# Transformer block with a routed feed-forward on one core: rate and waits of the indirect DMAs in the slots' stage

## The chip, the core and the metric

The kernel runs on one NeuronCore of a Trainium2 chip. The core has five instruction streams that run side by side and meet at semaphores: TensorE (PE, matmuls and transposes), VectorE (DVE), ScalarE (ACT), GpSimd (POOL) and SyncE (SP, which here issues the plain DMAs). Transfers are carried by 16 DMA engines that all queues share. The metric is the device time of one execution in microseconds (us). The kernel before takes 2183.7 us, the median of 12 runs from 2173.35 to 2190.69.

## What is computed

16 sequences of 512 tokens with 128 features pass through one block: layer norm with a modulation per sequence, causal attention with 16 heads of 8, and a feed-forward part with 160 experts of which each token uses 8. Cut to the part that the change bears on:

```python
logits = x @ router_w.T + expert_bias
probs = sigmoid(logits)
top_w, top_idx = top_k(probs, 8)
top_w = top_w / (sum(top_w) + 1e-09) * 2.5
combine = zeros((T, 160)).at[arange(T)[:, None], top_idx].set(top_w)
h1 = silu(einsum('th,eih->eti', x, w_gate))       # 64 inner features
routed = einsum('eti,ehi->th', h1 * combine.T[:, :, None], w_down)
shared = silu(x @ w_gate_shared.T) @ w_down_shared.T
return routed + shared
...
x = x + gb * ffn(h)
```

All arithmetic on the main path is in 32 bit; the scores of the attention use sums of bf16 parts.

## The kernel before

The kernel has two stages. In the first, up to about 1120 us of the profiled execution, it runs the attention of all 16 sequences, and behind it the routing: which expert gets which token, and in which place. In the second, the slots' stage, the experts are applied.

**Slots.** The sequences are taken in eight groups (`GROUPS = (2, 3, 3, 2, 2, 2, 1, 1)`). In each group every pair of experts gets blocks of 128 slots in two tensors in HBM: `xg`, the inputs by slot, and `yg`, the outputs by slot. Four blocks make a quad, and the stage works quad by quad, 28, 36, 36, 28, 28, 28, 22 and 22 of them by group, 228 in all (a few more of each group are kept in reserve and stand in a branch, `spare_quads`, L868 to L881, that every engine tests once a group at L870 and L874). For one quad SP loads `xs` from `xg` (L797), TensorE transposes it (`turn`), `up` multiplies by the first weights (`wq`, copied from a resident table by ACT and DVE, two blocks each), ACT applies silu, `down` multiplies by the second weights (`wd`, L814), ACT copies the result to `y`, and SP stores it to `yg` (L864).

**Indirect DMAs.** Two kinds go between tokens and slots, each with 128 rows of 512 bytes and each issued by GpSimd. A scatter (`scattering`, L752) writes 128 tokens' rows into `xg`; a sequence has 4 blocks of tokens times 8 choices, 32 of them, and all 16 have 512. A gather (`gathering`, L975) reads, for 128 tokens and one of their choices, the rows of `yg` into a slice of the tile `got`; there are 512 of these too. When the eight gathers of a block of tokens are there, `combine` (L987 to L999) weights and adds them on VectorE in six instructions, and after the fourth block SP stores the sequence to the output. `got` has five buffers (`LAG + 2`).

**What sets the order.** PE, SP, ACT and DVE run in the order of the source; GpSimd's side work and indirect DMAs are put into one order by `in_order`. Every indirect DMA also goes through `paced`, which adds a wait for `steps.last`, the matmul or transpose that stands last in the source at that point. In the attention the `Pacer` asks for one indirect DMA each 1.3 us of the planner's clock (`PACE`). In the slots' stage the loop at L1181 goes quad by quad; after each quad's steps it adds `RATE` to a debt (L1205) and issues one indirect DMA for each whole unit of it, scatters first, then gathers (L1207, `stream`). Nothing to issue sets the debt to zero. A group's gathers are put into the queue when the `down` of its last quad has been issued (L1200 to L1202). `add_up` (L1172) then issues the combines, keeping the three newest blocks back (`LAG`). `prepare_sums` (L1161) starts the shared expert (`shared_expert`, L886) and the top-8 weights (`weights`, L920) of the sequences whose gathers come next, on PE's tile `o`, ACT and DVE. What is left of the gathers after the last quad is issued by the loop at L1209.

`moe.sb` is None until the attention has ended, and is set at L1149, ahead of the quad loop.

Of the kernel before, what the change touches and what calls it, by code (L numbers as in the profile page):

```python
# [38 lines left out]
LAG = 3  # L39


PACE, RATE = 1.3, 2.3
PERIOD = 1.25


# [26 lines left out]
def block_kernel(ctx: ExitStack, tc: tile.TileContext, t: dict, out: bass.AP):  # L72
# [22 lines left out]
    steps = Steps()  # L95
# [128 lines left out]
    def in_order(ins):  # L224
        if behind:
            tc.add_manual_dep(ins, behind[-1].name, NO_SYNC, reason="order of issue")
        behind.append(ins)

    def paced(ins):

        if steps.last is not None:
            tc.add_manual_dep(ins, steps.last.name, SYNC, reason="pace")
        in_order(ins)

# [507 lines left out]
    def scattering():  # L742

        while True:
            while not next_rows:
                look_ahead()
                yield None
            gr, i, h = next_rows.popleft()
            look_ahead()
            for j in range(NBLK):  # L750
                for k in range(TOPK):
                    s = nc.gpsimd.indirect_dma_start(  # L752
                        out=gr.xg,
                        out_offset=bass.IndirectOffsetOnAxis(
                            ap=gr.idx[:, NBLK * i + j, k : k + 1], axis=0
                        ),
                        in_=h[:, j, :],
                        in_offset=None,
                    ).ins
                    tc.declare_no_dep(s, group=f"scatter{gr.g}", reason="every slot once")  # L760
                    tc.add_to_no_dep_group(f"scatter{gr.g}", s)
                    paced(s)
                    left[gr.g] -= 1
                    yield s
# [3 lines left out]
    moe = SimpleNamespace(sb=None)  # L768
# [198 lines left out]
    def gathering():  # L967

        while True:
            while not gathers:  # L970
                yield None
            gr, i, j = gathers.popleft()
            got = moe.sb.tile([P, TOPK, D], FP, tag="got", name="got", bufs=LAG + 2)
            for k in range(TOPK):
                s = nc.gpsimd.indirect_dma_start(  # L975
                    out=got[:, k, :],
                    out_offset=None,
                    in_=gr.yg,
                    in_offset=bass.IndirectOffsetOnAxis(
                        ap=gr.idx[:, NBLK * i + j, k : k + 1], axis=0  # L980
                    ),
                ).ins
                paced(s)
                yield s
            sums.append((gr, i, j, got))
# [445 lines left out]
```

## Time and profile before

| | |
|---|---|
| median of 12 runs | 2183.7 us (2173.35 to 2190.69) |
| the profiled execution | 2178.5 us |
| its span, first to last instruction | 2176.7 us |
| mean granted TensorE clock | 0.897 |
| busy, of the span: PE, DVE, ACT, POOL | 77%, 54%, 49%, 52% |
| scatters (L752): count, busy, mean of one | 512, 495.0 us, 967 ns |
| gathers (L975): count, busy, mean of one | 512, 511.4 us, 999 ns |
| first gather, last gather (start) | 1252.2 us, 2156.9 us |
| first and last `turn` transpose (start) | 1125.4 us, 1985.8 us |

Times in the trace are counted from the span's first instruction. "Busy" leaves out waiting. A row of a wait names who ended it: "A <- B" is time that A stood idle until B was done, as the profile infers it from the semaphores. The granted clock is what the throttle gave TensorE, as a share of full speed. The profile gives the DMA engines' load as the mean busy share of the 16. "issue" is time in which the engine waited for nothing that the profile shows.

### The profile page before, as it was taken

The page shows a single profiled execution, that of the slowest core. Times are in us where ns is not written, and L with a number is a line of the kernel's source. Part 1 is how long each engine was busy: PE and PEld are TensorE (multiplying, and loading weights), DVE is VectorE, ACT ScalarE, POOL GpSimd, SP SyncE. Part 2 cuts the span into 40 slices and gives each one's busy share as a digit, 9 for nine tenths or more (in the row PEclk, how much of TensorE's full clock was granted, in tenths as well). Part 3 has the DMA queues.
Part 4 walks back from the last instruction along what each step waited for, and adds up shares of the span by engine and source line. Part 5 has one row for each costly group of instructions (what it writes and reads, how often), then busy time and mean ns, then how long its engine had stood idle before and what let it go on. Part 6 is the DMA issues. An engine that isn't in the chain of part 4 may idle for free. (4 is left out here: it accounts for less than half of the span.)

```text
span 2176.7 us, 39288 instructions
## 1 busy us (share of the span) xinstructions
PE 1670.3 (77%) x12248; PEld 1127.2 (52%) x12248; DVE 1180.6 (54%) x3153; ACT 1066.8 (49%) x2031; POOL 1139.0 (52%) x1139
## 2 busy tenths in 40 slices
PE   2899987988879888788868888887978887887100
PEld 1455544544445444444447677676767676766000
DVE  2787776776667666565623313245454544454633
ACT  1466554654455444544556655555555555654000
POOL 4011066226654556666515555565666565656775
PEclk8899999998999898998989999999999999997555
DMA  3456555555555565565588788788888888887211
GB/s 98 130 178 187 165 182 176 175 167 169 185 183 168 180 212 166 172 196 178 180 276 265 249 260 275 250 271 288 271 266 281 266 281 263 293 266 234 82 56 43
DMA packets 298149, 445.30 MB, mean 205 GB/s; under 512 B 44923, under 2 KB 168796, under 8 KB 297920
## 3 DMA queue, kind: packets, MB, share of 16 engines
q1 hardware_dynamic: 265152, 375.32, 53.3%
q0 software_dynamic: 32768, 67.17, 10.7%
q8 instruction: 113, 1.85, 0.4%
q14 instruction: 116, 0.95, 0.1%
HBM read 223.37 MB, written 218.17 MB: 203 GB/s over the span
## 5 line engine op out<-in xcount | busy, mean ns | idle before, releaser
L752 POOL DMA_INDIRECT xg<-hs,idx x512 | 495.0, 967 | 401.1 <-PE s L105 146.2
L975 POOL DMA_INDIRECT got<-yg,idx x512 | 511.4, 999 | 288.7 <-issue 116.2
L1234 DVE TENSOR_REDUCE mins<-s 128x2 f32<-128x1024 f32 (+3 forms) x448 | 396.7, 912 | 231.4 <-PE s L105 174.3
L1234 ACT ACTIVATE pT<-s 128x1024 f32<-128x1024 f32 x320 | 322.0, 1021 | 254.8 <-PE s L105 180.8
L105 PE MATMUL down<-wd,su 128*128 x1824 | 274.0, 295 | 97.4 <-issue 46.3
L105 PEld LDWEIGHTS down<-wd,su 128*128 128x128 f32 x1824 | 229.7, 197 | 169.8 <-issue 106.8
L105 PE MATMUL up<-xT,wq 128*128 128x128 f32 x1824 | 257.5, 287 | 2.5 <-issue 2.5
L105 PE MATMUL s<-krep,qrep 96*128 96x512 bf16 (+3 forms) x1024 | 204.8, 314 | 67.0 <-issue 22.3
L105 PE MATMUL s<-qrep,krep 128*128 128x512 bf16 (+3 forms) x1024 | 202.5, 312 | 57.5 <-ACT pT L1234 25.2
L1234 DVE COPY wq<-wg 128x128 f32 x456 | 90.7, 251 | 278.4 <-PE up L105 179.2
L105 PEld LDWEIGHTS up<-xT,wq 128*128 128x128 f32 x1824 | 238.6, 204 | 2.6 <-issue 2.6
L105 PE MATMUL av<-pT,v 128*32 128x512 f32 (+3 forms) x2048 | 206.9, 470 | 0.6 <-issue 0.6
L1234 ACT ACTIVATE su<-up 128x512 f32<-128x512 f32 x228 | 137.4, 603 | 128.2 <-PE up L105 89.5
L1234 ACT COPY y<-down 128x512 f32<-128x512 f32 x228 | 133.4, 585 | 120.1 <-issue 35.9
L237 POOL TENSOR_TENSOR rot<-rot,three 128x512 f32<-128x512 f32 x32 | 36.7, 1159 | 279.3 <-ACT three L1234 279.1
L105 PEld LDWEIGHTS <-qrep 96*128 96x128 bf16 x1024 | 84.1, 100 | 175.4 <-issue 137.6
L105 PEld LDWEIGHTS <-identb 128*128 128x128 bf16 x1280 | 124.9, 102 | 89.6 <-issue 14.2
L1234 ACT COPY xT<-turn 128x512 f32<-128x512 f32 x228 | 133.2, 584 | 77.4 <-issue 26.3
L112 PE MATMUL turn<-ident,xs 128*128 128x128 f32 x912 | 148.6, 289 | 21.9 <-DMA xs<-xg 18.7
L105 PEld LDWEIGHTS <-krep 128*128 128x128 bf16 x1024 | 89.0, 100 | 104.8 <-issue 85.8
L1234 ACT COPY wq<-wg 128x128 f32 x456 | 114.1, 299 | 38.5 <-issue 21.5
L112 PEld LDWEIGHTS turn<-ident,xs 128*128 128x128 f32 x912 | 112.4, 149 | 39.3 <-issue 33.8
(174 smaller groups left out, 2218.8 us busy)
## 6 DMA issues: line engine op xcount, KB each, us to landing
xg<-zeros SPq DMA_DIRECT2D x288, 256.0 KB
xs<-xg SPq DMA_DIRECT2D x228, 256.0 KB
wd<-in_wdT SPq DMA_DIRECT2D x228, 256.0 KB
yg<-y SPq DMA_DIRECT2D x228, 256.0 KB
krep<-parts SPq DMA_DIRECT2D x64, 288.0 KB
qrep<-parts SPq DMA_DIRECT2D x192, 96.0 KB
yg<-zeros SPq DMA_DIRECT2D x60, 256.0 KB
parts<-three SPq DMA_DIRECT2D x96, 128.0 KB
```

The source lines that it names most:

```text
L105: steps.last = nc.tensor.matmul(out_, lhsT=lhsT, rhs=rhs, start=start, stop=stop).ins
L112: steps.last = nc.tensor.transpose(out_, in_, ident).ins
L237: in_order(getattr(nc.gpsimd, op)(*args).ins)
L752: s = nc.gpsimd.indirect_dma_start(out=gr.xg, out_offset=bass.IndirectOffsetOnAxis(ap=gr.idx[:, NBLK * i + j, k : k + 1], axis=0), in_=h[: ...
L975: s = nc.gpsimd.indirect_dma_start(out=got[:, k, :], out_offset=None, in_=gr.yg, in_offset=bass.IndirectOffsetOnAxis(ap=gr.idx[:, NBLK * i ...
L1234: return getattr(self.engine, op)(*args, **kwargs)
```

## The change

Two lines. The rate of the quad loop goes from 2.3 to 2.9 indirect DMAs a quad. And `paced` adds its wait for TensorE only while `moe.sb` is None, that is in the attention; in the slots' stage an indirect DMA keeps the order of its queue and its waits for data, and has no other.

```diff
-PACE, RATE = 1.3, 2.3
+PACE, RATE = 1.3, 2.9
...
     def paced(ins):
 
-        if steps.last is not None:
+        if moe.sb is None:
             tc.add_manual_dep(ins, steps.last.name, SYNC, reason="pace")
         in_order(ins)
```

## The prediction

> **What bounds the kernel now.** I read the slices of the page first, then busy time by stretches, then the waits of TensorE and GpSimd in the slots' stage, then the timeline of the end. The profiled execution took 2178.5 us around a span of 2176.7; the median of the 12 runs is 2183.7, 5.2 above it. The sum below is made in the span and carried to the median with 1.8 + 5.2 = 7.0.
>
> ```profile
> PE   2899987988879888788868888887978887887100
> POOL 4011066226654556666515555565666565656775
> ```
>
> Each digit is 54.4 us. From slice 20 on the slots run, with PE at 8 to 9 tenths and POOL at 5 to 6; in the last three slices PE is gone and POOL alone goes on at 7.
>
> ```profile
> core 0: us, PE busy (x) PEld busy (x) DVE busy (x) ACT busy (x) POOL busy (x), PEclk, DMA share, GB/s
> 1250.00:1990.00 740.00, 621.27 (x4369) 525.24 (x4368) 329.50 (x1010) 419.76 (x1015) 445.88 (x451) 0.95 0.84 271
> 1990.00:2115.00 125.00, 24.30 (x88) 15.57 (x86) 64.20 (x150) 7.39 (x15) 94.28 (x93) 0.52 0.30 89
> 2115.00:2177.00 62.00, 0.00 (x0) 0.00 (x0) 22.41 (x50) 0.00 (x0) 33.04 (x33) 0.50 0.15 44
> ```
>
> Between 1250 and 1990 PE is busy 84%, POOL issues 451 indirect DMAs, and the DMA engines are 84% busy. After 1990 there are 126 more, with PE and the DMA engines nearly idle: this end is GpSimd's alone.
>
> ```profile
> PE down L105 <- issue: 43.2, 43, 2.5
> PE down L105 <- ACT y L1234: 25.5, 18, 3.6
> PE down L105 <- DMA xs<-xg: 3.9, 2, 2.0
> PE up L105 <- DMA hides<-hide: 3.1, 2, 1.8
> PE down L105 <- DMA wd<-in_wdT: 2.2, 1, 2.2
> POOL got L975 <- PE up L105: 81.8, 66, 2.9
> ```
>
> These are waits in 1250 to 1990 (us in total, times, longest). TensorE lost about 10 us to transfers and none to a gather, so PE's own chain sets the stage. GpSimd lost 81.8 us in this line alone to the pacing wait. 784 `turn` matmuls, four a quad, lie in that stretch: 196 quads in 740 us, 3.78 us a quad.
>
> ```profile
> 1991.38 11.41 SPq L864 DMA_DIRECT2D yg<-y  x4
> 2005.93 0.94 POOL L975 DMA_INDIRECT got<-yg,idx  x1 [1.73 <-PE o L112]
> 2115.79 0.94 POOL L975 DMA_INDIRECT got<-yg,idx  x1 [0.30 <-DVE got L1234]
> 2156.85 0.94 POOL L975 DMA_INDIRECT got<-yg,idx  x1 [0.31 <-issue]
> 2141.12 1.23 DVE L1234 TENSOR_TENSOR got<-got,w 128x1024 f32<-128x1024 f32 x1
> 2149.51 1.23 DVE L1234 TENSOR_TENSOR got<-got,w 128x1024 f32<-128x1024 f32 x1
> 2166.31 1.23 DVE L1234 TENSOR_TENSOR got<-got,w 128x1024 f32<-128x1024 f32 x1
> 2169.78 1.22 DVE L1234 TENSOR_TENSOR got<-got,w 128x1024 f32<-128x1024 f32 x1
> ```
>
> Start, duration, idle before and what ended it. The instruction list has 116 gathers behind the last branch of L874. The trace has 116 starts from 2005.93 to 2156.85, so these are they: 1.31 us each, back to back. The last 32, from 2115.79, belong to the last group, whose results were all sent by 2002.8. They wait for nothing but the 84 gathers of older groups in front of them. A combine, the six VectorE instructions from one of these DVE lines to the next, takes 8.4 us at 2141 and 3.5 at 2166.
>
> **The change, part by part.** The instruction list of the changed kernel can be read without running it. Up to the slots' stage nothing differs, and there are as many matmuls, copies and DMAs in all. Behind the last branch stand 32 gathers, not 116. The other 84 move into the stage, with the shared expert (L886) and the weights (L920) of the last batches and their combines. All indirect DMAs from the start of the stage on lose their wait on PE and keep those on data: the landing of the group's `yg`, a free `got` buffer (five), the indirect DMA eight before.
>
> *The end.* The first gather of group 7 now needs only its `yg`. At the first group's end such a gather began at 1252.2, 5.9 us after its last `yg` DMA had been issued (to 1246.3). So here it begins at 2002.8 + 5.9 = 2008.7. The 32 then take what they take now up to the last start, 2156.85 - 2115.79 = 41.1, to 2049.8; 2 us to land; one combine of 3.5 to 8.4, since DVE has 10 us a block and is no longer two combines late; 3.5 us for the output, as from 2173.2 to 2176.7 now. That is 2059 to 2064; I take 2062, a gain of 115. If DVE stays as late as now, the span ends 60.9 behind the first of the 32, at 2069.6: 107.
>
> *TensorE.* The moved shared experts are 48 matmuls. At the end they take 17.33 us on a clock of 0.52; in the stage 72 such take 14.39 us, 0.20 each.
>
> ```profile
> 1750.00:1990.00 240.00, 14.39 (x72) 8.88 (x72) 3.43 (x5) 5.80 (x13) 0.96 0.86 277
> 1990.00:2115.00 125.00, 17.33 (x48) 9.65 (x48) 2.06 (x3) 4.33 (x9) 0.52 0.30 89
> ```
>
> (Columns as above for tile `o`, without POOL.) 48 x 0.20 = 9.6 us, all on the path, since PE sets the stage. Bounds: 0, if they fall into PE's gaps, and 17.3. ACT's share, 4.3 us, lies under PE at 57% busy. DVE gets some 60 us more (86.6 at the end now, less about 26 that stay); 329.5 of 740 rises by seven points to about 52%, hidden behind PE. Should that cover go, the price is one combine, 3.5 us, ahead of the `wq` copies, which are written two quads before their use: still hidden.
>
> *The DMA engines.*
>
> ```profile
> q1 hardware_dynamic: 265152, 375.32, 53.3%
> q0 software_dynamic: 32768, 67.17, 10.7%
> ```
>
> 10.7% of 2176.7 over 1024 indirect DMAs is 0.227 us of all 16 engines each: 84 x 0.227 = 19.1. Loads and stores of the moved batches, about 3.2 MB at 53.3% x 2176.7 / 375.32 = 3.09 us a MB, add 9.9. These 29 us go into an idle share of 0.16 x 740 = 118. If hidden they cost nothing; if the engines are the bound, 29. Nearest row: the 10 us that PE now waits for transfers. Idle share falls by a quarter, so I take 4 us more.
>
> *GpSimd.* A gather in the stage is 384.08 us / 387 = 0.99 us, and the next begins 0.30 later: 1.29. 2.9 x 1.29 = 3.74 us a quad against 3.78. It just keeps up while there is work (the first five groups, 156 of 228 quads). By the tail's 1.31 it is 3.80, 0.02 x 156 = 3 us late; I take 3. What is behind a late gather: the next gathers, then the combine, three blocks (24 gathers, 31 us) later in the list, then on DVE the `wq` copies and on SP the output at L999 and the loads behind it. The far end is the longest gather of the stage, 1.90 + 0.30; that is the slower rival.
>
> The wait itself I cost at nothing: a full GpSimd is behind PE's place, so pacing holds it seldom. The cover is that fullness; in groups 5 to 7 the list runs empty and only data holds it.
>
> The Trainium skill speaks against the change here: "SBUF — State Buffer", section "SBUF: two separate sides", says that VectorE's 32-bit copies inside SBUF lock GpSimd out of writing DMA descriptors. The two `wq` copies a quad (0.227 us median each) would add 0.45 us to 2.9 x 1.244 = 3.61, making 4.06 and costing 0.28 x 156 = 44 us. The rows of this case show a mean of 0.99 over a median of 0.944, 0.05 a gather, and the sum goes by them.
>
> Sum of the span: 2176.7 - 115 + 9.6 + 4 + 3 = 2078.3. With 7.0 for the median: about 2085.
>
> **Rivals.**
> *The forecast, about 2085, chance 0.68.* For it: PE waits for no gather, and the last 32 stand behind older ones.
> *Half is given back, chance 0.22.* DMA engines at 84% already have slices of nine tenths, so the added work could be fully exposed: 17.3 + 29 in place of 9.6 + 4, and a gain of 107 at the end. 2176.7 - 107 + 17.3 + 29 + 3 + 7 = 2126. Against it: only 10 us of PE's waits are for transfers.
> *Late gathers hold TensorE, slower, chance 0.08.* GpSimd falls behind by more than 31 us, the combine waits at the head of DVE, `wq` comes late, PE runs at GpSimd's rate. It decides from 2.9c = 3.78 + 98 / 156 (98 being what the rest gains, 115 less 9.6, 4 and 3), c = 1.52 us a gather. At c = 1.65 it is 4.79, 1.01 x 156 = 157 us: 2085 + 157 = 2242. For it: single gathers of 1.9, unpaced bursts. Against: bursts of five in the trace hold 1.25 to 1.3.
> *The waits' removal and the rate cancel, no change, chance 0.02.* Were the list emptied only on paper, GpSimd would keep its 0.61 DMAs a us, 451 / 740, and the 84 end as late as now: 2184. Against: 81.8 us of its waits are the pace.
>
> **How the numbers follow.** The low end is zero cost in the stage with the full 117 at the end: 2183.7 - 117 = 2067, rounded out to 2064. The high end is the half-back case with the gather at 1.31 and DVE late by one combine more, 2126 + 8 = 2134, to 2136. That leaves out the slower rivals and a little of each edge. A change within 0.3%, 6.5 us, can't be told from none. Faster: 0.68 + 0.22 = 0.90; same 0.02; slower 0.08.
>
> **What would show it.** Behind the last branch 32 starts of `got`, not 116, and PE's last matmul about 60 us before the end in place of 107. POOL at 7 tenths or more over slices 23 to 34, with no wait on PE there. PE's stage longer by 10 to 25 us. The prediction is wrong if a DVE wait on `got` stands in the stage, if a gather's mean there passes 1.2 us, or if PE's waits for `xs`, `wd` and `hides` grow past 40 us.

## The result, and the profile after

The changed kernel takes 2551.1 us (median of 15 runs, 2527.2 to 2561.3) beside 2180.6 us for the kernel before (62 runs), a ratio of 1.1695 [1.1672, 1.1718]. It is slower by 370 us, where 2085 us, a gain of about 99, was forecast. The profiled execution has a span of 2545.1 us at a mean granted clock of 0.830; before it was 2176.7 us at 0.897.

The page after, its rows of busy tenths (40 slices of 63.6 us):

```profile
PE   3899889888887788857460981865766666647561
POOL 3111462466266566533446036344444444554414
PEclk8899989998999899978785985877877778877776
```

Up to the slots' stage, which begins in the 18th slice, the rows are nearly those of before. From there on PE mostly has 4 to 7 tenths, in two slices 0 and 1, and the clock falls with it. GpSimd is not fuller but emptier: mostly 3 to 5 tenths where 7 were foreseen.

One view cut to windows of 20 us in the stage of the changed kernel (columns: window, length, busy time and instructions of PE, PEld, DVE, ACT and POOL, granted clock, DMA share, GB/s):

```profile
1320.00:1340.00 20.00, 1.19 (x8) 0.78 (x6) 0.89 (x3) 1.18 (x2) 15.29 (x16) 0.59 0.22 73
1340.00:1360.00 20.00, 1.89 (x9) 1.89 (x10) 0.00 (x0) 1.08 (x3) 15.19 (x16) 0.50 0.22 64
1360.00:1380.00 20.00, 2.81 (x14) 2.05 (x13) 0.00 (x0) 0.59 (x1) 15.12 (x16) 0.59 0.26 80
1380.00:1400.00 20.00, 0.00 (x0) 0.00 (x0) 0.36 (x2) 0.60 (x1) 8.51 (x9) 0.50 0.12 33
1400.00:1420.00 20.00, 17.77 (x127) 16.04 (x128) 3.68 (x19) 13.68 (x32) 0.00 (x0) 0.86 0.73 230
1420.00:1440.00 20.00, 20.00 (x147) 16.51 (x145) 3.36 (x16) 14.70 (x35) 0.00 (x0) 1.00 0.81 255
```

While GpSimd issues 16 indirect DMAs in 20 us, one every 1.25 us, matmuls, DVE and ACT together have under 4 us of work in the 20. When GpSimd holds still, PE is busy for 18 to 20 us at once. The DMA engines are not full in the first four windows, 0.12 to 0.26. So the stop is no lack of DMA bandwidth.

How a stop begins, in the timeline of the changed kernel (start, duration, instruction, and in brackets the idle time before it):

```profile
1136.07 0.96 POOL L752 DMA_INDIRECT xg<-hs,idx  x1 [0.30 <-issue]
...
1136.19 0.23 PE L105 MATMUL s<-digits,onesb 1*128 1x160 bf16 x1
1137.33 0.96 POOL L752 DMA_INDIRECT xg<-hs,idx  x1 [0.30 <-issue]
...
1144.60 0.82 DVE L1234 TENSOR_TENSOR key<-s,m 128x640 f32<-128x640 f32 x1 [13.20 <-issue]
```

The DMA at 1136.07 is the sixth of a run that began at 1129.74. DVE needs only the `s` that PE ended at 1136.4, and starts 8 us later.

The instructions by which SP issues the loads of `wd` (L814; duration in ns, minimum, median, maximum), of the changed kernel in the window 1355 to 1395:

```profile
L814 SPq FUSED_REGOPS  x1: 700/700/700, 1363.0 to 1363.0; - x1
L814 SPq MOVE wd<-in_wdT x1: 688/688/688, 1365.8 to 1365.8; - x1
```

Over the whole execution the median of the first is 37 ns, of the second 29. In these stretches a step of SP's sequencer, one that moves no data, takes 0.69 to 0.70 us. The kernel before has such steps too (its longest `FUSED_REGOPS` at L814 takes 703 ns). Of all 456 such steps at L814 in the changed kernel, 24 of the 71 that begin behind the sixth or a later indirect DMA of an unbroken row take 0.68 us or more, and 2 of the 385 others.

The longest waits of the changed kernel between 1125 and 2490 us (sum, times, longest):

```profile
DVE wq L1234 <- remote: 419.3, 32, 57.2
POOL got L975 <- DVE xr L1234: 371.1, 32, 66.2
...
PE down L105 <- ACT y L1234: 276.7, 36, 38.6
```

"remote" is a release that the profile can't name. The second row is GpSimd at the end of its runs (a run is a row of indirect DMAs with no gap to speak of between them): with no other wait it runs ahead until all five buffers of `got` are full, and is held by data alone. Its whole list of waits for PE, 81.8 us on `up` before, is gone as the change says.

### The profile page after: what moved, and what is told of

It reads as the page before. It is cut to its first block, busy times and chain, and to the rows that moved or that the text cites. A ratio compares the mean times of both kernels' runs of the same rounds, so it can differ in the third digit from the quotient of the medians.

```text
span 2545.1 us, 39051 instructions
## 1 busy us (share of the span) xinstructions
PE 1760.0 (69%) x12248; PEld 1209.1 (48%) x12248; DVE 1170.5 (46%) x3153; ACT 1082.5 (43%) x2031; POOL 1125.3 (44%) x1139
## 5 line engine op out<-in xcount | busy, mean ns | idle before, releaser
L975 POOL DMA_INDIRECT got<-yg,idx x512 | 496.3, 969 | 632.7 <-DVE xr L1234 371.1
L105 PE MATMUL down<-wd,su 128*128 x1824 | 316.5, 326 | 446.5 <-ACT y L1234 277.4
L105 PEld LDWEIGHTS down<-wd,su 128*128 128x128 f32 x1824 | 267.3, 225 | 521.2 <-ACT y L1234 294.8
L105 PE MATMUL up<-xT,wq 128*128 128x128 f32 x1824 | 282.5, 304 | 12.7 <-issue 12.1
L105 PEld LDWEIGHTS up<-xT,wq 128*128 128x128 f32 x1824 | 264.4, 222 | 9.1 <-issue 8.3
L112 PE MATMUL turn<-ident,xs 128*128 128x128 f32 x912 | 168.6, 316 | 41.1 <-DMA xs<-xg 19.3
L112 PEld LDWEIGHTS turn<-ident,xs 128*128 128x128 f32 x912 | 128.1, 165 | 68.2 <-issue 38.6
```

The costliest lines, as they stand in the source:

```text
L105: steps.last = nc.tensor.matmul(out_, lhsT=lhsT, rhs=rhs, start=start, stop=stop).ins
L112: steps.last = nc.tensor.transpose(out_, in_, ident).ins
L975: s = nc.gpsimd.indirect_dma_start(out=got[:, k, :], out_offset=None, in_=gr.yg, in_offset=bass.IndirectOffsetOnAxis(ap=gr.idx[:, NBLK * i ...
```

## The experiments

The experiments stand in four groups, and every result is a ratio to the kernel before, timed in the same group. The results name the chip. The first group ran on chip 4, where the kernel before took 1998 us; the second on chip 5 (2180 us); the third and fourth on chip 15 (2194 and 2196 us). Beside the runs of the changed kernel above it took 2181 us; the chip of those is not named. In brackets stands a 95% interval.

### One part of the change at a time, chip 4 (before: 1998.1 us)

The wait for PE's place given back, the rate kept:

```diff
-        if moe.sb is None:
+        if steps.last is not None:
```

> Rate 2.9 with the wait on TensorE kept. Theory A (it is GpSimd running ahead with nothing to hold it that stops the other engines, and the wait was what held it): the tail shrinks as forecast and nothing stops, 2085 to 2110 us. Theory B (the rate: back-to-back indirect DMAs stop the other engines whatever they wait for, and at 2.9 a quad they are back to back): slower than before, 2300 to 2550 us. Theory C (more gathers in the stage make DVE wait for late data): 2200 to 2400 us, with DVE waits on got in the stage.

Measured: 1908.2 us, 0.956 [0.952, 0.961].

The old rate, without the wait:

```diff
-PACE, RATE = 1.3, 2.9
+PACE, RATE = 1.3, 2.3
```

> Rate 2.3 without the wait on TensorE. Theory A: the gathers still go in bursts of eight and more, ahead of their place, so the other engines stop as in the changed kernel: 2400 us or more. Theory B: at 2.3 a quad there is idle time between them, so the stage stays as it was and the time is 2170 to 2200 us. Theory C: as B.

Measured: 1980.9 us, 0.992 [0.990, 0.995].

In two more, scatters keep the wait and each gather waits instead for the landing of the gather four (or three) before it. In this and the later diffs "..." stands for lines that are left out: `paced` gets a second argument, `gather`, which only the gathers set, and the lists begin empty.

```diff
...
-        if moe.sb is None:
+        if moe.sb is None or gather is None:
             tc.add_manual_dep(ins, steps.last.name, SYNC, reason="pace")
+        elif len(ring) >= 4:
+            tc.add_manual_dep(ins, ring[-4].name, SYNC, reason="depth")
+        if gather:
+            ring.append(ins)
...
```

> Rate 2.9, scatters wait for TensorE, a gather in the slots' stage waits for the landing of the gather four before it in place of TensorE (the semaphore lanes alone allow eight). Theory A in the form that the number of indirect DMAs handed over and not yet landed decides, with a threshold between four and eight: 2080 to 2120 us. Theory B, and theory A in the form that any run of gathers ahead of their place stops the others: 2400 us or more.

> As the run with four, with the gather three before it. Theory A by number in flight: no stops if four had none, and if four had some, fewer; three in some 4 us (0.96 to issue, 0.3, 2.7 to land) are 1.33 us a gather, about full rate, so 2090 to 2150 us. Theory B: as the run with four, 2400 us or more.

Measured: 0.979 [0.974, 0.984] and 1.0225 [1.0175, 1.0275].

In these runs the loss is not there. The same step at L814, of the kernel with rate 2.9 and the wait kept, is never slow:

```profile
L814 SPq FUSED_REGOPS  x228: 37/37/51, 1022.0 to 1845.9; - x114
```

The same 37/37/51 stands in all four traces, the one without the wait among them, in which GpSimd's longest run has 122 indirect DMAs without a break (gaps under 0.5 us). A depth of three holds GpSimd itself, which is why it loses; the gathers' row of that kernel on its page:

```profile
L979 POOL DMA_INDIRECT got<-yg,idx x512 | 523.2, 1022 | 289.3 <-DMA got<-yg,idx 178.9
```

There, late gathers do what the prediction's slower rival said. None of the theories on the wait could be decided here; their times in us were set for a kernel before of 2180 us.

### The changed kernel again, and the wait by kind of DMA (before: 2179.7 us)

The changed kernel without an edit, then the kernel with the wait and the new rate of above:

> The changed kernel itself, once more, beside the kernel before of the same call. Two theories are left after four runs in which the kernel before took 1998 us, where it had taken 2181 us beside the changed kernel's 2551 us. Theory C (the chip): the stop of the other engines comes on chips that are slower already under the kernel before, and unheld GpSimd only sets it off there. Then, if before takes about 2000 us in this call, the changed kernel takes 0.94 to 0.99 of it (the kept-wait kernel's 0.956, and the 0.992 of the kernel without wait at the old rate, set its ends), the register operations of line 814 last 37 ns with a longest of about 50, and DVE's wq copies wait for no more than they did; if before takes about 2180 us, the changed kernel is at 1.15 or more again, with register operations of 700 ns. Theory R (the combination): rate 2.9 with no wait fills GpSimd's queue without a gap, and does so on any chip. Then the ratio is 1.15 or more whatever before takes, and line 814 shows 700 ns.

Measured: 2548.5 us, 1.170 [1.165, 1.175], and `FUSED_REGOPS` at L814 again goes up to 700 ns.

> The kernel before with 2.9 in place of 2.3, the wait for TensorE's place kept. Theory C and theory R alike: 0.95 to 0.965 of before where before takes 2000 us. Where before takes 2180 us: theory C, 0.95 to 0.98, since GpSimd is held through the stage and only its last 32 gathers run unheld; theory R the same. A ratio over 1.0 there would say that the rate alone, with no wait removed, already brings the loss, and both theories would be short of a cause.

Measured: 2192.9 us, 1.0067 [1.0040, 1.0093]. The two differ by the wait alone, and by 356 us. And the rate alone, 4.4% faster on chip 4, gains nothing here. It is above both theories' 0.95 to 0.98.

The wait for the gathers only, then for the scatters only:

```diff
...
-        if moe.sb is None:
+        if moe.sb is None or gather:
...
```

> The changed kernel with the wait given back to the gathers alone; scatters wait for data alone. In the trace of the changed kernel the first stop, from 1136.2 us on, came in a run of scatters. If unheld issue of any kind is the cause (theory C on a chip where before takes 2180 us, theory R on any), the stops come in the runs of scatters and the ratio lies between the kept-wait kernel's and the changed kernel's, 1.03 to 1.13. If the gathers are the cause, through their writes or through the combines that wait for them, 0.95 to 0.97. On a chip where before takes 2000 us theory C says 0.95 to 0.98.

```diff
...
-        if moe.sb is None:
+        if moe.sb is None or not gather:
...
```

> The changed kernel with the wait given back to the scatters alone; gathers wait for data alone. If unheld issue of any kind is the cause, the ratio lies between the kept-wait kernel's and the changed kernel's, 1.03 to 1.13, and what this one and the one with held gathers lose adds up to about what the changed kernel loses. If only scatters do it, 0.95 to 0.97; if only gathers do it, 1.13 or more. On a chip where before takes 2000 us theory C says 0.95 to 1.0.

Measured: 1.045 [1.042, 1.048] with free scatters, 1.130 [1.125, 1.136] with free gathers. Beside 1.0067 that is 0.038 and 0.123, together 0.162; free of both costs 1.170 - 1.007 = 0.163. The two add up, and the stage has 128 scatters and 512 gathers, so that each costs about the same (0.030 and 0.024 per hundred): the cost is a matter of how much is issued unheld, whichever way the data go. The 1.045 lies in the 1.03 to 1.13 expected of unheld issue of any kind. The 1.130 stands at its edge, where "only gathers" begins; that one is ruled out by what the scatters cost. Whether the chip or the combination decides was still open, as this chip is one of the slower ones.

### Pauses, and a rate between (before: 2193.6 us)

Four small memsets of GpSimd after every fourth indirect DMA of the stage; as many, but 24 after every 24th; and the first with the wait kept:

```diff
...
         in_order(ins)
+        if moe.sb is not None:
+            issued.append(ins)
+            if len(issued) % 4 == 0:
+                for _ in range(4):
+                    side("memset", moe.pause, 0.0)
...
```

> The changed kernel, with four small memsets of GpSimd (128x64 f32, 213 ns each in the trace of before) put after every fourth indirect DMA of the slots' stage. It gives GpSimd 144 x 0.85 = 123 us more to do and takes no wait back. Theory U (unbroken runs): GpSimd's indirect DMAs, when more than about five follow each other 0.30 us apart, bring the other engines to a crawl on this chip, and a gap of about 1 us ends it. GpSimd then needs 576 x 1.29 + 123 = 866 us for the stage, which stands at 1122 us, with a tail of some 100: 2090 to 2260 us where before takes 2180, ratio 0.96 to 1.04, against the changed kernel's 1.17, though GpSimd has more to do. Theory L (lateness: what costs is that GpSimd, without TensorE's place, is late with gathers and scatters or works at the wrong time): 1.17 or more. Where before takes 2000 us, U says about 0.98: no crawl to be taken away, and GpSimd's 4.36 us per quad set the stage.

> The same memsets, as many of them, but 24 together after every 24th indirect DMA: the same added work of GpSimd, with runs of 24 left whole. Theory U: the runs crawl as in the changed kernel, 1.12 to 1.20 where before takes 2180 us. A theory in which only GpSimd's pace counts (the memsets slow it, and a slower GpSimd does less harm) expects the same as for pauses after every fourth, within 0.03. Where before takes 2000 us: about 0.98, both.

> The kernel before with 2.9 in place of 2.3, TensorE's place kept, and the memsets after every fourth indirect DMA. Without the memsets it was at 1.0067 where before took 2180 us. In its trace 65 of its runs had six indirect DMAs or more, and TensorE was busy for 0.62 of the time behind the sixth, against 0.95 behind the second to fourth. Theory U: the sixth DMA's loss goes, but GpSimd's 4.36 us per quad are more than TensorE's 3.78, so it falls behind and its waits are passed: 0.98 to 1.04, near the changed kernel with the same pauses. A result at 1.10 or more says that U is short of something.

Measured: 1.101 [1.095, 1.107], 1.166 [1.160, 1.172] and 1.010 [1.006, 1.015]. With the same added work the short runs are 141 us faster than the long ones, and faster than the changed kernel. So more work for GpSimd can save time, and GpSimd's pace alone, which is the same in both, is not the cause. But the first was expected at 1.04 at most. Its trace shows two reasons. In the stage's scatters the memsets came to stand one behind each DMA, inside the 0.3 us that lie between two DMAs anyway, and those runs stayed whole. And among the gathers, which do come in fours with pauses of 0.94 us or more, the pause is too short. A stretch of such fours (columns as in the windows above):

```profile
1360.00:1380.00 20.00, 10.76 (x65) 9.42 (x65) 1.88 (x10) 6.62 (x16) 15.22 (x27) 0.76 0.53 169
1380.00:1400.00 20.00, 10.37 (x44) 9.27 (x44) 0.88 (x3) 3.35 (x8) 15.68 (x30) 0.67 0.43 129
1400.00:1420.00 20.00, 6.02 (x26) 5.50 (x27) 1.34 (x7) 4.03 (x11) 13.21 (x24) 0.59 0.26 80
```

Where fours of gathers follow each other with gaps under 1.5 us, a matmul is recorded for 0.91 to 0.96 of the time behind the DMAs of the first four, for 0.64 to 0.79 in the second and for 0.54 to 0.65 from the fourth four on. So theory U's "a gap of about 1 us ends it" is wrong: the loss builds up over short runs too, when they follow each other closely. The third came out as expected, and no faster than without the pauses.

The kernel before with 2.6 in place of 2.3:

> The kernel before with 2.6 in place of 2.3, TensorE's place kept. 58 of the 116 gathers behind the last branch move into the stage, 58 x 1.31 = 76 us off the end. Theory U where before takes 2180 us: issue leaves 3.78 - 2.6 x 1.29 = 0.43 us free per quad, half of before's 0.81, so runs grow longer in part: 0.97 to 1.0. A theory in which the rate costs in proportion (rate 2.9 gave back all of its 116 us) expects 1.0. Where before takes 2000 us: 0.96 to 0.98.

Measured: 2179.1 us, 0.993 [0.990, 0.996]. It lies in theory U's range and close to the 1.0 of the other theory, so it decides little between them. It has the lowest ratio of all that ran where the kernel before takes 2180 to 2196 us. Where before takes 1998 us, 2.9 with the wait (0.956) has; 2.6 was not run there.

### Length of the runs, or number in flight (before: 2196.5 us)

Once more the old rate without the wait; then the depth of four; then, with the scatters held, every fifth and every twelfth gather waiting for the landing of the one before it:

```diff
...
-        if moe.sb is None:
+        if moe.sb is None or not gather:
             tc.add_manual_dep(ins, steps.last.name, SYNC, reason="pace")
+        elif issued and len(issued) % 5 == 0:
+            tc.add_manual_dep(ins, issued[-1].name, SYNC, reason="landed")
+        if gather:
+            issued.append(ins)
...
```

> The changed kernel with 2.3 in place of 2.9: the wait is gone, the rate is the old one. Theory W (the wait alone): without it GpSimd runs on as far as data and its own buffers let it, at either rate, so where before takes 2180 us the ratio is that of the changed kernel within 0.05, 1.12 to 1.20. Theory X (it needs both): GpSimd has its 0.81 us free per quad and mostly keeps to them: 0.99 to 1.05. Where before takes 2000 us it was 0.992 and both expect that again.

> The changed kernel; scatters wait for TensorE's place as before, a gather waits for the landing of the gather four before it, so no more than four are in flight. A gather landed 2.5 to 2.8 us after its issue in the trace of before, and four issues take 5.2 us, so the runs are rarely broken. Beside the one with held scatters and free gathers (1.130 where before takes 2180 us): theory U (unbroken runs) 1.06 to 1.14; theory F (too many in flight) 0.99 to 1.03. Where before takes 2000 us it was 0.979, and both expect that again.

> The changed kernel; scatters wait for TensorE's place as before, and every fifth gather waits for the landing of the gather before it, which leaves a gap of some 1.6 us: (2.5 to 2.8 from issue to landing, less 0.95 of issue). Theory U: runs of no more than five, so little of the crawl: 0.98 to 1.05 where before takes 2180 us. Theory F: the number in flight falls to none only once in five, 1.06 to 1.12. Where before takes 2000 us: 0.95 to 1.0.

> The same with every twelfth gather. Theory U: behind the fifth to sixth issue of a run TensorE was busy for 0.3 to 0.5 of the time instead of 0.9, so a run of twelve loses about seven issues of 1.29 us in part: 1.06 to 1.12 where before takes 2180 us, between the one that breaks at five and the 1.130 of free gathers. If it is as good as breaks at five, within 0.01, the length of the runs is not what counts. Where before takes 2000 us: 0.95 to 0.99.

Measured: without the wait at 2.3, 1.161 [1.155, 1.167]; depth four, 1.130 [1.124, 1.135]; breaks at five, 1.047 [1.042, 1.052]; breaks at twelve, 1.098 [1.091, 1.104].

Taking the wait out costs 359 us at the old rate, as much as at the new one, so it needs no combination (theory W, not X). At 2.3 the same kernel gained on chip 4, so the cost goes with the chip (theory C), or with something else that set those runs apart: chip 4 ran one group only. No more than four gathers in flight helps nothing (1.130, as with free gathers; theory F falls). Runs cut at twelve win back a quarter of the 0.123 that free gathers cost, runs cut at five two thirds. The gathers' rows on the pages of the kernels that break at five, and that have a depth of four:

```profile
L979 POOL DMA_INDIRECT got<-yg,idx x512 | 505.3, 987 | 433.7 <-DMA got<-yg,idx 279.7
```

```profile
L979 POOL DMA_INDIRECT got<-yg,idx x512 | 493.6, 964 | 571.4 <-DVE xr L1238 345.1
```

In the first, GpSimd stands for 280 us waiting for its own gathers to land, and the kernel is 178 us faster than the second. There it isn't held by landings, runs ahead, and stops at the full buffers like the changed kernel. The breaks at five have a price of their own: PE waits 87 us for `wq`, since DVE stands at late gathers for 307 us. That is about the 0.040 that this kernel stays above the one with the wait; whether it is the same time was not tested. Nor did these runs separate the length of a run from the number of DMAs in a given time: the median gap between two runs of gathers is 2.8 us here, and 0.94 us in the kernel with a pause after every fourth.

The same seen within the traces. A run is here a row of indirect DMAs with less than 0.5 us from the end of one to the start of the next, from the attention's end to the last 32 gathers. The table gives the share of the 1.25 us from the start of a run's n-th DMA in which a matmul is recorded (in brackets the number of such DMAs):

```
kernel (before's time)              2nd    4th    5th    6th        7th        8th        16th
wait kept, rate 2.9    (2180 us)    0.98   0.93   0.88   0.62 (65)  0.70 (13)  0.48 (11)  -
changed kernel again   (2180 us)    0.91   0.92   0.70   0.40 (40)  0.24 (40)  0.28 (40)  0.11 (18)
gathers break at 5     (2196 us)    0.89   0.81   0.72   0.50 (14)  0.20 (2)   -          -
gathers break at 12    (2196 us)    0.88   0.90   0.69   0.49 (50)  0.36 (42)  0.34 (41)  -
depth of four          (2196 us)    0.95   0.86   0.58   0.38 (52)  0.34 (37)  0.26 (36)  0.19 (13)
pause after every 4th  (2194 us)    0.72   0.71   0.43   0.31 (6)   0.17 (6)   0.17 (6)   0.33 (3)
no wait, rate 2.3      (1998 us)    0.94   0.84   0.92   0.93 (20)  0.89 (20)  0.88 (20)  0.88 (13)
```

In the first five rows, of chips 5 and 15, PE keeps 0.81 or more up to the fourth, and falls from the fifth or sixth on. With short pauses it is at 0.72 already behind the second. On chip 4 it does not fall: there the kernel with the wait and rate 2.9 has an unbroken run of 541 and is the fastest of all.

## Why the prediction was wrong, step by step

**The wait, costed at nothing: the step that failed.** "The wait itself I cost at nothing: a full GpSimd is behind PE's place, so pacing holds it seldom." Taking it out costs 356 us at the new rate and 359 at the old one. The premise was wrong by itself: in the stage of before, 146 of GpSimd's pauses, 241 us in all, end with PE, and the 81.8 us that the prediction shows are one row of these. With rate 2.9 and the wait kept there are still 105, with 207 us; the largest row for the gathers in that kernel:

```profile
POOL got L975 <- PE up L105: 70.3, 52, 2.8
```

These pauses cut the runs: in the stage of before all but 8 of 155 runs had five DMAs or fewer, which is about as many as these chips bear. Without them the changed kernel has 41 runs of six or more, up to 69 long, and its stage takes 487 us more than the 882 of before (below):

```profile
1121.00:2490.00 1369.00, 841.88 (x5197) 709.15 (x5197) 429.25 (x1347) 522.63 (x1207) 594.71 (x612) 0.77 0.56 178
```

And the argument asked what the pauses do to GpSimd, not what GpSimd does to the others when nothing holds it. The evidence offered against a slowdown, "bursts of five in the trace hold 1.25 to 1.3", looked at GpSimd's own time, which stays the same in the longest run; the damage is on the other engines.

Before's own tail, 116 gathers in one run, had shown it in part. A combine early in that run, and the middle of one late in it:

```profile
2045.10 1.23 DVE L1234 TENSOR_TENSOR got<-got,w 128x1024 f32<-128x1024 f32 x1 [4.39 <-DMA got<-yg,idx]
2046.36 1.48 DVE L1234 TENSOR_TENSOR got<-got 128x512 f32<-128x512 f32 x3
2047.88 0.29 DVE L1234 TENSOR_TENSOR got<-got,gate 128x128 f32<-128x128 f32 x1
...
2143.54 0.69 DVE L1234 TENSOR_TENSOR got<-got 128x512 f32<-128x512 f32 x1 [1.19 <-DVE got L1234]
2144.94 0.43 DVE L1234 TENSOR_TENSOR got<-got 128x256 f32<-128x256 f32 x1 [0.71 <-DVE got L1234]
2146.35 0.29 DVE L1234 TENSOR_TENSOR got<-got 128x128 f32<-128x128 f32 x1 [0.98 <-DVE got L1234]
2147.74 0.29 DVE L1234 TENSOR_TENSOR got<-got,gate 128x128 f32<-128x128 f32 x1 [1.10 <-DVE got L1234]
```

Late in the run DVE's instructions take as long as ever but start 1.40 us apart, twice the 0.70 us of SP's slow steps, and a combine takes 8.3 to 12 us in place of 3.4. The prediction took the 8.4 and the 3.5 as a range and did not ask why they differ. Yet the first six combines of that tail, some 40 gathers into the run, take 3.4 us, and so do the four among the last 32 gathers of the changed kernel. So a long run is not enough by itself; what more it takes was not shown.

**The rate's cost in the stage: sized at 17 us (9.6 + 4 + 3), measured at about 130.** Rate 2.9 with the wait kept shows the step by itself. The stage of before and of that kernel (columns as in the windows above):

```profile
1121.00:2003.00 882.00, 734.45 (x5159) 618.24 (x5159) 376.09 (x1192) 504.66 (x1201) 522.09 (x527) 0.94 0.83 267
```

```profile
1121.00:2130.00 1009.00, 794.78 (x5181) 665.21 (x5179) 433.24 (x1343) 506.80 (x1205) 607.70 (x612) 0.89 0.75 240
```

The stage is 127 us longer by these windows; the second ends 5 us ahead of its last `y` (2135.2 us), so it is 133 if both are taken to the last `y`. PE has 22 matmuls more, as the trace has them, and is busy 60 us longer, while the clock falls from 0.94 to 0.89 (by itself that would be 734 x 0.94 / 0.89 - 734 = 41 us, an estimate). The other 67 us are waiting (214 us against 148), on ACT's `y` (67.4 against 33.6) and on "issue" (75.4 against 46.3, in the rows of `down`). The 65 runs that reach a sixth DMA lose about 65 x 1.25 x 0.3 = 24 us at the sixth, an estimate from the table; what takes the rest was not separated. The DMA share did not rise but fell, from 0.83 to 0.75, so full DMA engines are not what holds it, and the rival with half given back named the wrong cost. On chip 4 the same stage takes 830 us with 735.5 of PE, so it is no cost of the work itself.

**The gain at the end: right.** The kernel with the wait and rate 2.9 has 32 starts behind the last branch, as forecast, and its last matmul stands 53 us before the end of the span instead of 107, where 60 was forecast. Behind the windows above, 173.7 us were left before and 58.3 are now, a gain of 115 as forecast (121, if both are counted from the last `y`). In the changed kernel 38 gathers start after GpSimd has passed the last branch, six that stand ahead of it in the list and the 32, and its last matmul also stands 53 us before the end.

**VectorE's copies locking GpSimd out: rightly left out of the sum.** The mean gather of the changed kernel is 969 ns, of the one with the wait 995, of before 999. In the trace of before, 51 gathers share over 0.1 us with a `wq` copy and with nothing else of DVE: their mean is 944 ns, that of the 147 without any such neighbour 943. The long ones stand beside the first multiplication of a combine, `got<-got,w`: 36 gathers with it alone have a mean of 1404 ns and reach 1917. They make up over half of the 0.05 us a gather.

**The rivals.** "Removal and rate cancel" (2184) gives the size of the rate alone, 2193, for another reason: the 84 gathers do come earlier, and the stage pays for it. "Late gathers hold TensorE" had the right sign and the wrong place. Its mechanism, DVE at a late combine and PE behind it at `wq`, stands in the kernels with a depth of three (82 us of PE's waits), with breaks at five (87 us), and, on chip 4, with a depth of four (35 us). In the changed kernel it is under 1 us: PE's waits are for ACT's `y`, and the longest of ACT and DVE for releases that the profile can't name.

**What would show it.** Of the signs that were to show the prediction wrong, none came: the gather's mean stayed under 1.2 us, PE's waits for `xs`, `wd` and `hides` did not grow, and no DVE wait on `got` for a landing stands in the stage. Of those that were to show it right, POOL's seven tenths and the 10 to 25 us of PE's stage failed. The sign that mattered, all engines idle at once while one runs at its full rate, was not on the list.

**What stays open.** Why a sequencer step takes 0.70 us behind a run of indirect DMAs was not shown, nor why the runs on chip 4 are free of it, nor whether the length of a run or the number of DMAs in some microseconds decides. The changed kernel itself was not run on chip 4; its two halves there, 0.956 and 0.992, suggest that it would gain.

## What to carry to other kernels

A wait that looks like lost time of its own engine can be what protects the others: before taking it out, add up all its rows, look in the trace for a place where that engine already runs unheld, and see what everybody else does there. Read a stretch by windows of all engines, not by the waits of one: idle everywhere with one engine at its full rate and the DMA engines far from full was here neither a wait for data nor a lack of bandwidth. Where indirect DMAs are many, try a cap on how many are issued in a row, with breaks longer than the 0.94 us that did not suffice here, and time it on more than one chip.

## What the runs showed of the hardware

- In the slots' stage, behind the fifth or sixth of GpSimd's indirect DMAs 0.30 us apart, on chips 5 and 15, PE's busy share went from 0.9 to 0.3. Of SP's steps behind the sixth or later, 24 of 71 took 0.68 us or more, most of them 0.69 to 0.71, in place of 0.03 to 0.04 (changed kernel). A wait for one landing at every fifth gather won back two thirds of what free gathers cost; pauses of 0.94 us after every fourth did not stop the loss.
- GpSimd itself does not slow: in the stage of the changed kernel an indirect DMA of 128 rows of 512 bytes takes 0.99 us on average up to the fifth of a run and 0.96 behind it. The medians are 0.944 to 0.947 us for a gather and 0.958 to 0.962 for a scatter, on all three chips.
- DVE's 32-bit copies of 128 x 128 inside SBUF (`wq`) did not lengthen a gather (944 ns beside one, 943 without); gathers beside its multiplication `got<-got,w` took 1404 ns.
- The same program took 1998 us on chip 4 and 2180 to 2196 us on chips 5 and 15, and the sign of an edit changed with it: the old rate without the wait is 0.992 on the one and 1.161 on chip 15.
- The granted clock was low where PE stood idle: 0.50 to 0.59 in the windows of 20 us with under 3 us of PE, 0.86 and 1.00 in the two with 18 and 20; 0.77 over the stage of the changed kernel, 0.94 before.
